# Two handovers from routed experts to wide-headed attention: rooms of the gathers, order of the first two tiles, place of a weight product

## The chip, the core and the metric

The kernel runs on one core of a Trainium2 chip. A core has five engines that work side by side: TensorE (PE in the profile; its weight loads are PEld), VectorE (DVE), ScalarE (ACT), GpSimd (POOL) and SyncE (SP), which here only issues transfers. Each engine takes its instructions in order from a queue of its own. Sixteen DMA engines move data between the device memory and the on-chip memory. The metric is the device time of one execution in microseconds; smaller is better.

## What is computed

The reference is a network of four layers over 16 sequences of 64 tokens with 256 features (1024 token rows), with a context of 1024 keys of 192 features per sequence. Each layer has a cross attention to the context, a mixing step along the sequence and a feed-forward part, each added to `x`:

```python
x = x + _L1_ffn_ref(_layernorm(x), ...)     # 8 experts, each token goes to one
x = x + _L2_xattn_ref(_layernorm(x), ctx)   # 8 heads of 64
x = x + _L2_attn_ref(_layernorm(x), ...)    # a linear recurrence
x = x + _L2_ffn_ref(_layernorm(x), ...)     # 8 experts, each token goes to two
x = x + _L3_xattn_ref(_layernorm(x), ctx)   # 8 heads of 64
x = x + _L3_attn_ref(_layernorm(x), ...)    # a state-space layer
x = x + _L3_ffn_ref(_layernorm(x), ...)     # three dense products
```

Two pieces matter here. A routed layer adds to each token the outputs of its experts, weighed by gates. And the state-space layer maps its input `u` to a step size through two matrices one after the other:

```python
x_dbl = u @ x_proj_w
delta, b, c = jnp.split(x_dbl, [D_INNER, D_INNER + D_STATE], axis=-1)
delta = jax.nn.softplus(delta @ dt_proj_w + dt_proj_b)
```

The first 512 columns of `x_proj_w` (called xT, transposed) and `dt_proj_w` (dt), both 512 x 512, can be multiplied with each other once, without any token. The kernel does that: this is the weight product.

## The kernel before

The 1024 token rows lie on chip as `xs`, eight tiles of 128 rows (NT = 8); a tile holds two sequences. The layers run one after the other; the two cross attentions with eight heads of 64 (L2 and L3) share one routine, `heads64` (line 420), and each is woven with the sequence layer that follows it: L2 with a recurrence, L3 with the state-space layer (`state_space`, line 1779).

*Experts to attention.* In a routed layer (`L1_ffn`, `L2_ffn` at line 1397) each expert's output rows `yb` are written to a buffer `ys` in the device memory, on ACT's DMA queue (lines 1328 and 1460). Nothing is added to `xs` there. The attention that follows does it, tile by tile, in `carry` (line 1306): for each chosen expert it allocates a tile, gathers 128 rows of `ys` into it with an indirect DMA on POOL's queue (line 1304), and adds them, times the gate, to `xs` on DVE (line 1313). After L1's experts a tile has one such gather, after L2's experts two. In `heads64` the gathers' room has the tag `o` with one buffer, the same buffer that then holds the tile's normalized rows (lines 450 and 452).

*`heads64`.* `output_matrices` (line 429) multiplies value and output weights per head. `normalized(i)` (line 449) carries tile i, normalizes it (statistics on DVE, a power on POOL at line 160, scaling on DVE at line 453), transposes it on TensorE (line 179) and copies the result (`hT`). `queries(i)` (line 458) multiplies `hT` by the query weights and scales them to `qT` on DVE (line 465). `with_keys(i, n)` (line 472) multiplies the queries by the key weights, for n = 0 and 1, and copies the result to `qp`. Then come 32 steps, each a tile, one of its two sequences and half of the heads: `scores` (line 500) makes two 128 x 1024 score tiles, `exp_rows` takes their maxima on DVE (line 223) and exponentials on ACT (line 225) into tiles of the tag `p` (two buffers of 1024 numbers per row), which later steps transpose and average. Before the change the prologue runs in this order:

```python
            output_matrices()
            for i in range(2):
                normalized(i)
            queries(0)
            for n in range(2):
                with_keys(0, n)
```

Tiles 2 and on are normalized inside the steps, two tiles ahead.

*What sets the order.* TensorE's instructions run in the order in which the program writes them (`manual_schedule`). The other engines' queues are ordered by a scheduler that works with estimated times, so an instruction may stand well ahead of its place in the program. It keeps data and rooms: a tile whose tag has all buffers taken waits until an older one has had its last reader.

*Between the steps.* `heads64` calls `breathe(place)` four times a step, which is the `go` function of the neighbouring layer. In L3 the state-space layer's first piece of work is `weights()` (line 1806): its first call takes the weights, the next four make one quarter each of the weight product, xT by dt on TensorE (line 1813), which a copy on ACT puts in xT's place (line 1814). So two quarters run before the first scores and two behind them. `prepare` (line 1817) uses the product once two tiles have left the attention.

*Weights.* Weights are loaded into a ring of two slots (`slot`, `carve`, `load` at line 131, on SP's queue); `pack` hands out a slot and starts the loads of the next. `pack_L3_attn` (line 1733) loads five matrices of the state-space layer when the last L2 expert has left its slot: in, xT, dt (1024 KB each), bc (64 KB) and out (512 KB). Each L2 expert's weights are three loads of 1024 KB. The pool `act` has two rooms of 8 KB per row, `htok` and `hT`, which hold the normalized tokens and their transpose while `L2_ffn` routes; in L3 `hT` next holds `up` (line 1831) and `htok` holds `bc_rep`.

Of the kernel before, what the change touches and what calls it, by code (L numbers as in the profile page):

```python
# [11 lines left out]
F32 = mybir.dt.float32  # L12
# [30 lines left out]
class Net:  # L43
# [373 lines left out]
            nc.sync.dma_start(ck, self.a["ctx"][b])  # L417
        return cT, ck

    def heads64(self, large=None, breathe=lambda place: None, finished=lambda i: None):  # L420


        nc = self.nc
# [23 lines left out]
                self.evict(wvo2[:, 2 * g : 2 * g + 2], ps)  # L447

        def normalized(i):
            self.carry(i, "o", 1)  # L450
            mv, rs = self.norm_tile(self.xs[:, i, :], 1e-5)
            o = self.lp.tile([128, D], F32, tag="o", bufs=1, name="o")
            nc.vector.tensor_scalar(o, self.xs[:, i, :], mv[:, 0:1], rs, ALU.subtract, ALU.mult)
            nc.gpsimd.tensor_tensor(self.xs[:, i, :], self.xs[:, i, :], bo, ALU.add)
            hT[i] = self.lp.tile([128, 2, 128], F32, tag="hT", bufs=2, name="hT")
            self.evict(hT[i], self.transposed(o))
# [15 lines left out]
        def with_keys(i, n):  # L472

            qT, qp = qpT[i]
            ps = [large([128, 4, 2, S]) for _ in range(2)]
            for hp in range(4):
                for r in range(2):
                    rows = slice(64 * r, 64 * r + 64)
                    self.mm(
                        ps[r][:, hp].rearrange("p b q -> p (b q)"),  # L480
                        [(wkT[rows, hp, 128 * n : 128 * n + 128], qT[rows, hp, :])],
                    )
            for r in range(2):
# [49 lines left out]

        with self.tc.manual_schedule(engines={mybir.EngineType.PE}):
            output_matrices()
            for i in range(2):
                normalized(i)
            queries(0)
            for n in range(2):
                with_keys(0, n)  # L540
            steps = [(i, par, g) for i in range(NT) for par in range(2) for g in range(2)]
            one = two = None
            for k in range(len(steps) + 2):
                x = steps[k] if k < len(steps) else None
                now = None
                if x is not None:
                    i, par, g = x
                    if not par and not g:
                        onT = [
                            self.lp.tile([128, 8, 2, S], F32, tag="onT", bufs=1, name="onT"),  # L550
                            self.lp.tile([128, 4, 2, S], F32, tag="onT2", bufs=1, name="onT2"),
                        ]
                    if not g:
                        ctx = self.fetch_cut_ctx(2 * i + par)
                    now = {"x": x, "ctx": ctx, "onT": onT}
                breathe(0)
# [12 lines left out]
                breathe(3)  # L569
                if two is not None:  # L570
                    by_features(on, two["onT"], two["x"][1], 2 * two["x"][2] + 1)
                if one is not None:
                    one["on"] = averages(one["pT"][0], one["sums"][0], one["ctx"][1])
                if two is not None and two["x"][1:] == (1, 1):
                    output(two["x"][0], two["onT"])
                    finished(two["x"][0])
                if now is not None and (par, g) == (0, 1):
                    if i + 2 < NT:
                        normalized(i + 2)
                    if i + 1 < NT:  # L580
                        queries(i + 1)
                one, two = now, one
# [720 lines left out]
    def gather_rows(self, out, src, at):  # L1303
        return self.nc.gpsimd.indirect_dma_start(out, None, src, bass.IndirectOffsetOnAxis(ap=at, axis=0))

    def carry(self, i, tag="back", bufs=2):

        if self.routed is None:
            return
        for at, g in zip(self.routed.at, self.routed.gates):  # L1310
            y = self.lp.tile([128, D], F32, tag=tag, bufs=bufs, name="back")
            self.gather_rows(y, self.ys, at[:, i : i + 1])
            self.nc.vector.scalar_tensor_tensor(
                self.xs[:, i, :], y, g[:, i : i + 1], self.xs[:, i, :], ALU.mult, ALU.add
            )
# [81 lines left out]
    def L2_ffn(self):  # L1397
# [31 lines left out]

        for e in range(E):  # L1430
            w1, w2, w3 = self.pack()
            dT = self.lp.tile([128, 2, CAP], F32, tag="dT", bufs=2, name="dT")
            for v, (s0, n) in enumerate(L2_CUTS):
                hb = self.lp.tile([n, D], F32, tag=f"hb{n}", bufs=2, name="hb")
# [296 lines left out]


    def pack_L3_attn(self):
        self.slot()
        return tuple(self.load(f"L3a_{n}") for n in ("in", "xT", "dt", "bc", "out"))

    def pack_L3_ffn(self):
        t = self.ring.tile([128, 4 * RING], U8, tag="w", name="w")
# [8 lines left out]
    def L3(self, ctx_pool):  # L1747
        tc, nc = self.tc, self.nc
        with ExitStack() as stack:
# [10 lines left out]
            with (  # L1760
                tc.tile_pool(name="sb_L3x", bufs=1, side="left", reuse_waits="tile") as self.lp,
                tc.tile_pool(name="ps_L3x", bufs=1, space=PSUM, reuse_waits="tile") as self.lps,
            ):
                self.heads64(
                    lambda shape: self.lps.tile(shape, F32, tag="t", bufs=2, name="large"),
                    ssm.go, ssm.more,
                )
            ctx_pool.__exit__(None, None, None)
            self.lp = pool("sb_L3f", bufs=1, side="left")
# [9 lines left out]
    def state_space(self):  # L1779
        nc = self.nc  # L1780
        N = 16
        w = []
# [20 lines left out]
            s.xn += 1  # L1803
            return s.x[s.xn % 6]

        def weights():
            w.extend(self.pack(ahead=False))
            yield

            for k in range(4):  # L1810
                cols = slice(k * 128, (k + 1) * 128)
                ps = self.lps.tile([128, 4, 128], F32, tag="t", bufs=2, name="large")
                self.mm(ps.rearrange("p m f -> p (m f)"), [(w[1][:, r, cols], w[2][:, r, :]) for r in range(4)])
                nc.scalar.copy(w[1][:, :, cols], ps)
                yield

        def prepare(k):
            win, wdt, _, wbc, _ = w
            ug = ugs[k % 2]
            os = []  # L1820
            for t in range(2):
# [66 lines left out]
            return got  # L1888

        def items(k):  # L1890
            wout = w[4]
            ug = ugs[k % 2]

            bc = self.act.tile([128, 2, 4, CHUNK], F32, tag="htok", name="bc_rep")
# [83 lines left out]
        def more(i):  # L1978
            s.ready = i + 1

        s.go, s.more = go, more
        s.x = rooms(self.sb, "x", 6)
        s.rep = rooms(self.sb, "rep", 4)
        s.xn = s.repn = 0
# [321 lines left out]
```

## Time and profile before

| | us |
|---|---|
| median of 3 runs | 3025.43 |
| lowest and highest | 3025.0, 3040.91 |
| the profiled execution | 3029.32 |
| its span | 3027.5 |
| TensorE busy, of the span | 2704.1 (89%) |
| VectorE busy | 1482.0 (49%) |
| ScalarE busy | 1022.6 (34%) |
| GpSimd busy | 309.4 (10%) |
| mean granted TensorE clock | 0.942 |

The page gives busy time by engine, the span in forty slices, and the chain of work that ended last, followed back from the last instruction to whatever released each step. The other views used below are the timeline (instructions in order of time, with the idle time of the engine before each and what ended it) and windows (busy time of every engine in a stretch, the granted clock, the share of the DMA engines and their rate). Times in them are counted from the span's start. The handover from L1's experts to L2's attention lies at about 1302 to 1331 us, the one from L2's experts to L3 at about 2025 to 2090 us.

### The profile page before, as it was taken

Reading aid. Unit: us, or ns where it says so; the run is one execution under the profiler, and the core shown is the slowest. Engines: PE = TensorE matmul, PEld = TensorE weight load, DVE = VectorE, ACT = ScalarE, POOL = GpSimd, SP = SyncE. Lnnn points to the kernel's source line nnn. Section 1 sums busy time; section 2 is a strip of 40 time slices with the busy share of each in tenths; the row PEclk is TensorE's granted clock in tenths of the full one; section 3 lists DMA queues with packets and bytes.
Section 4 is the critical chain, followed back from the end, with each engine's and each line's share of the span. In section 5 each row is a group of like instructions: output and inputs, shape, how many; then the busy total and the mean of one; then the engine's idle time right before and its main releaser. Section 6 shows DMA issues by size and latency. Waiting matters only on the chain.

```text
span 3027.5 us, 42618 instructions
## 1 busy us (share of the span) xinstructions
PE 2704.1 (89%) x16840; PEld 1955.0 (65%) x16840; DVE 1482.0 (49%) x3177; ACT 1022.6 (34%) x2290; POOL 309.4 (10%) x428
## 2 busy tenths in 40 slices
PE   7888997999999787979999997887998898887899
PEld 3566784666666346857777776874766666665668
DVE  3654115666666643234444344223445657658581
ACT  2331122555555111223333321122335455455330
POOL 1112223000000112310101011201001000000000
PEclk9997997999999897989999998998999999998999
DMA  9504771101010004811111113450212212121110
GB/s 242 171 27 159 253 230 51 36 26 36 26 36 22 28 9 171 281 49 54 55 44 47 60 42 116 163 217 22 67 43 84 74 51 83 56 67 53 57 36 7
DMA packets 79220, 253.55 MB, mean 84 GB/s; under 512 B 15151, under 2 KB 26954, under 8 KB 69290
## 3 DMA queue, kind: packets, MB, share of 16 engines
q1 hardware_dynamic: 59562, 165.01, 17.5%
q0 software_dynamic: 13312, 80.28, 7.8%
q10 hardware_dynamic: 6144, 5.51, 0.5%
q8 instruction: 134, 2.20, 0.3%
q14 instruction: 68, 0.56, 0.1%
HBM read 233.80 MB, written 14.82 MB: 82 GB/s over the span
## 4 chain that ended last, share of the span: by engine, by line
PE 64%; DVE 11%; ACT 4%; DMA 3%; issue 3%; POOL 1%; SPq 1%; ACTq 0%; DVEq 0%; POOLq 0%
PE misc L69 11%; PE sc L500 8%; PE halves L69 7%; PE gu L69 5%; PE misc L235 4%; PE ps_h L69 4%; PE po L69 4%; PE ps_t L235 3%; PE sc L69 2%; PE misc L864 2%; ACT p L225 2%; PE o L915 2%; PE misc L878 2%; DMA back<-ys,route_at 2%; DVE x L1926 2%
## 5 line engine op out<-in xcount | busy, mean ns | idle before, releaser
L223 DVE TENSOR_REDUCE nmx<-sc 128x1 f32<-128x1024 f32 x264 | 311.6, 1218 | 234.9 <-PE sc L500 150.4
L225 ACT ACTIVATE p<-sc,nmx 128x1024 f32<-128x1024 f32 x264 | 294.6, 1116 | 312.1 <-DVE nmx L223 311.4
L500 PE MATMUL sc<-ctxT,qp 128*128 128x512 f32 (+1 forms) x1024 | 353.4, 599 | 0.0
L500 PEld LDWEIGHTS sc<-ctxT,qp 128*128 128x128 f32 (+1 forms) x1024 | 137.8, 189 | 153.0 <-issue 151.6
L69 PE MATMUL halves<-ctx,pT 128*128 128x192 f32 x1024 | 191.0, 343 | 9.4 <-DVE xs L89 4.0
L69 PEld LDWEIGHTS halves<-ctx,pT 128*128 128x128 f32 x1024 | 178.4, 203 | 12.3 <-DVE xs L89 4.5
L160 POOL TENSOR_TENSOR ln_rs<-ln_ve,nhalf 128x1 f32<-128x1 f32 x120 | 67.0, 563 | 1142.3 <-DVE ln_ve L158 1081.6
L69 PE MATMUL misc<-ctx,pT 128*128 128x192 f32 x1024 | 177.6, 327 | 0.5 <-DVE qT L465 0.5
L69 PEld LDWEIGHTS misc<-ctx,pT 128*128 128x128 f32 x1024 | 166.3, 191 | 2.1 <-DVE qT L465 1.0
L235 PE MATMUL ps_t<-ident,p 128*128 128x128 f32 x1088 | 147.2, 277 | 21.9 <-ACT p L225 14.0
L1916 ACT ACTIVATE da<-rep,al 128x252 f32<-128x252 f32 x256 | 114.7, 498 | 115.0 <-DVE x L1926 95.6
L1926 DVE TENSOR_TENSOR_SCAN x<-da,x 128x512 f32<-128x512 f32 x128 | 151.9, 1210 | 1.9 <-ACT da L1916 1.4
L235 PE MATMUL misc<-ident,p 128*128 128x128 f32 x1024 | 139.8, 283 | 14.1 <-ACT p L225 6.7
L237 ACT COPY pT<-ps_t 128x512 f32<-128x512 f32 x182 | 104.3, 585 | 139.3 <-PE ps_t L235 137.3
L235 PEld LDWEIGHTS ps_t<-ident,p 128*128 128x128 f32 x1088 | 127.1, 143 | 36.0 <-ACT p L225 17.7
L235 PEld LDWEIGHTS misc<-ident,p 128*128 128x128 f32 x1024 | 112.2, 143 | 40.2 <-ACT p L225 13.3
L69 PE MATMUL ps_h<-r,w 128*128 128x256 f32 x512 | 115.3, 385 | 0.0
L237 ACT COPY pT<-misc 128x512 f32<-128x512 f32 x128 | 75.0, 586 | 114.9 <-PE misc L235 114.6
L69 PEld LDWEIGHTS ps_h<-r,w 128*128 128x128 f32 x512 | 97.8, 192 | 16.6 <-issue 2.9
L69 PE MATMUL gu<-dT,wa 128*128 128x128 f32 (+1 forms) x864 | 104.7, 280 | 3.7 <-ACT dT L64 2.4
L239 DVE COPY pT<-misc 128x512 f32<-128x512 f32 x128 | 88.2, 689 | 39.4 <-PE misc L235 28.9
L69 PE MATMUL po<-wb,hid 128*128 128x256 f32 (+1 forms) x440 | 105.9, 388 | 0.2 <-ACT hid L1380 0.2
(468 smaller groups left out, 4449.5 us busy)
## 6 DMA issues: line engine op xcount, KB each, us to landing
ctx<-in_ctx SPq DMA_DIRECT2D x48, 768.0 KB
ctxT<-in_ctxT SPq DMA_DIRECT2D x48, 512.0 KB
w<-in_L2f_W SPq DMA_DIRECT2D x24, 1024.0 KB
rep<-dus SPq DMA_DIRECT2D x256, 64.0 KB
ctxT<-in_ctxT SPq DMA_DIRECT2D x16, 768.0 KB
ctxT<-in_ctxT SPq DMA_DIRECT2D x96, 128.0 KB
ys<-yb ACTq DMA_DIRECT2D x40, 128.0 KB
bc_rep<-bcs SPq DMA_DIRECT2D x32, 128.0 KB
```

The source lines that it names most:

```text
L69: self.nc.tensor.matmul(out, lhsT, rhs, start=n == 0, stop=n == len(pairs) - 1)
L160: nc.gpsimd.tensor_tensor(rs, ve, self.nhalf, ALU.pow)
L223: self.nc.vector.tensor_reduce(nmx, sc, AX.X, ALU.max, negate=True)
L225: self.nc.scalar.activation(p, sc, AF.Exp, bias=nmx, accum_out=sums)
L235: self.nc.tensor.transpose(ps[:, u, :], p[:, at : at + 128], self.ident)
L237: self.nc.scalar.copy(pT[:, 4 * g : 4 * g + 4, :], ps)
L239: self.nc.vector.tensor_copy(pT[:, 0:4, :], ps)
L500: nc.tensor.matmul(sc[u][:, bass.ts(kh, 512)], qp[n][par][rows, h : h + 2, :].rearrange("p h q -> p (h q)"), ctx[0][rows, at], start=n == ...
L864: nc.tensor.matmul(ps[kh], wk[:, kh, cols], cT[:, bass.ts(kh, 512)], start=True, stop=False)
L878: nc.tensor.matmul(ps[kh][:, u, :], cT[:, 512 * kh + at : 512 * kh + at + 128], wv[:, 0, :], start=u == 0, stop=False,)
L1916: nc.scalar.activation(da[:, g, :, 1:], now[j][:, 0, :].rearrange("p (b s) -> p b s", s=S)[:, :, 1:], AF.Exp, scale=al[:, col : col + 1],)
L1926: nc.vector.tensor_tensor_scan(flat, da.rearrange("p g b s -> p (g b s)"), flat, 0.0, ALU.mult, ALU.add)
```

## The change

Four edits, cut to their core:

1. `carry` can be given a room. For the first two tiles of `heads64` the gathers go into a tile of the exponentials' tag `p`, seen as four rows of 256, each expert's rows in a part of its own. Tiles from the third on keep the tag `o` with one buffer.
2. In the prologue tile 1 is normalized behind tile 0's queries and their products with the keys, instead of ahead of them.
3. `heads64` calls a new hook, `first`, between the output matrices and tile 0. In L2 it does nothing. In L3 it makes the whole weight product, which was spread over the first steps.
4. xT and dt are loaded in `L2_ffn`, in the program's place of the fourth expert, into the rooms `htok` and `hT` of the pool `act`. `pack_L3_attn` only carves its slot; in, bc and out are loaded by the first call of `weights()`. The slot no longer has a part for dt.

```diff
         def normalized(i):
-            self.carry(i, "o", 1)
+            if i < 2:
+                self.carry(i, self.lp.tile([128, 4, D], F32, tag="p", bufs=2, name="p"))
+            else:
+                self.carry(i, tag="o", bufs=1)
...
             output_matrices()
-            for i in range(2):
-                normalized(i)
+            first()
+            normalized(0)
             queries(0)
             for n in range(2):
                 with_keys(0, n)
+            normalized(1)
...
-    def carry(self, i, tag="back", bufs=2):
+    def carry(self, i, room=None, tag="back", bufs=2):
...
-        for at, g in zip(self.routed.at, self.routed.gates):
-            y = self.lp.tile([128, D], F32, tag=tag, bufs=bufs, name="back")
+        for n, (at, g) in enumerate(zip(self.routed.at, self.routed.gates)):
+            y = self.lp.tile([128, D], F32, tag=tag, bufs=bufs, name="back") if room is None else room[:, n, :]
...
         for e in range(E):
             w1, w2, w3 = self.pack()
+            if e == 3:
+                self.early = [
+                    self.act.tile([128, 4, 512], F32, tag=tag, name=name)
+                    for tag, name in (("htok", "w_xT"), ("hT", "w_dt"))
+                ]
+                for w, n in zip(self.early, ("xT", "dt")):
+                    nc.sync.dma_start(w, self.a[f"L3a_{n}"])
...
     def pack_L3_attn(self):
         self.slot()
-        return tuple(self.load(f"L3a_{n}") for n in ("in", "xT", "dt", "bc", "out"))
+        shape = {n: self.a[f"L3a_{n}"].shape for n in ("in", "bc", "out")}
+        return self.carve(*shape["in"]), self.carve(128, 4, 512), self.carve(*shape["bc"]), self.carve(*shape["out"])
...
-        def weights():
+        def first():
             w.extend(self.pack(ahead=False))
-            yield
-
+            x, dt = self.early
             for k in range(4):
                 cols = slice(k * 128, (k + 1) * 128)
                 ps = self.lps.tile([128, 4, 128], F32, tag="t", bufs=2, name="large")
-                self.mm(ps.rearrange("p m f -> p (m f)"), [(w[1][:, r, cols], w[2][:, r, :]) for r in range(4)])
+                self.mm(ps.rearrange("p m f -> p (m f)"), [(x[:, r, cols], dt[:, r, :]) for r in range(4)])
                 nc.scalar.copy(w[1][:, :, cols], ps)
-                yield
+
+        def weights():
+            for n, to in zip(("in", "bc", "out"), (w[0], w[2], w[3])):
+                nc.sync.dma_start(to, self.a[f"L3a_{n}"])
+            yield
```

More of the change, by code (lines that the diff above doesn't have):

```diff
@@ L418, in fetch_cut_ctx, with heads64 @@
         return cT, ck
-    def heads64(self, large=None, breathe=lambda place: None, finished=lambda i: None):
+    def heads64(
+        self, large=None, breathe=lambda place: None, finished=lambda i: None, first=lambda: None
+    ):
         nc = self.nc
@@ L1765, in L3 @@
                     lambda shape: self.lps.tile(shape, F32, tag="t", bufs=2, name="large"),
-                    ssm.go, ssm.more,
+                    ssm.go, ssm.more, ssm.first,
                 )
@@ L1812, in weights @@
                 ps = self.lps.tile([128, 4, 128], F32, tag="t", bufs=2, name="large")
[L1813 removed]
+                self.mm(ps.rearrange("p m f -> p (m f)"), [(x[:, r, cols], dt[:, r, :]) for r in range(4)])
                 nc.scalar.copy(w[1][:, :, cols], ps)
[L1815 removed]
+        def weights():
+            for n, to in zip(("in", "bc", "out"), (w[0], w[2], w[3])):
+                nc.sync.dma_start(to, self.a[f"L3a_{n}"])
+            yield
         def prepare(k):
[L1818 removed]
+            win, wdt, wbc, _ = w
             ug = ugs[k % 2]
@@ L1890, in items @@
         def items(k):
-            wout = w[4]
+            wout = w[3]
             ug = ugs[k % 2]
@@ L1979, in more @@
             s.ready = i + 1
-        s.go, s.more = go, more
+        s.go, s.more, s.first = go, more, first
         s.x = rooms(self.sb, "x", 6)
```

## The prediction

> **What bounds the kernel now.** I read the page's busy line and chain first, then the chain in order of time, which points at two stretches where no matmul is on it, and then the timeline of those two.
>
> ```profile
> PE 2704.1 (89%) x16840; PEld 1955.0 (65%) x16840; DVE 1482.0 (49%) x3177; ACT 1022.6 (34%) x2290; POOL 309.4 (10%) x428
> ...
> PE 64%; DVE 11%; ACT 4%; DMA 3%; issue 3%; POOL 1%; SPq 1%; ACTq 0%; DVEq 0%; POOLq 0%
> ```
>
> TensorE is busy 89% of the span and carries 64% of the chain that ends last, so microseconds in which it stands idle, or does work that fits into an idle stretch, are what an edit can win. Two such stretches lie where a routed layer hands over to attention. The timeline of the second (L2's experts to L3):
>
> ```profile
> 2030.05 1.94 PE L69 MATMUL large<-w 64*64 64x256 f32 x16 [0.71 <-DVE w L62]
> ...
> 2036.07 0.97 POOL L1304 DMA_INDIRECT back<-ys,route_at  x1 [76.02 <-DMA w<-in_L3a_bc]
> ...
> 2039.58 0.94 POOL L1304 DMA_INDIRECT back<-ys,route_at  x1 [2.54 <-DVE xs L1313]
> ...
> 2044.99 0.69 PE L179 MATMUL halves<-ident,o 128*128 128x128 f32 x2 [13.00 <-DVE o L453]
> ...
> 2054.88 0.69 PE L179 MATMUL halves<-ident,o 128*128 128x128 f32 x2 [9.20 <-DVE o L453]
> ...
> 2055.36 3.62 PE L69 MATMUL large<-hT,w 128*128 128x128 f32 x16
> ...
> 2063.16 0.48 DVE L1313 SCALAR_TENSOR_TENSOR xs<-back,route_g,xs 128x256 f32<-128x256 f32 x1 [3.35 <-DMA back<-ys,route_at]
> ...
> 2067.43 9.88 PE L69 MATMUL large<-w 128*128 128x512 f32 x16 [0.59 <-ACT qp L64]
> ...
> 2077.15 5.51 PE L500 MATMUL sc<-ctxT,qp 128*128 128x512 f32 x16
> ...
> 2082.59 7.13 PE L69 MATMUL large<-w 128*128 128x512 f32 x16
> ```
>
> Columns: start, duration, engine, line, output<-input, and in brackets the idle time and its releaser. The output matrices end at 2031.99. TensorE then waits 13.00 us for tile 0's normalized rows and 9.20 us for tile 1's, and only then multiplies queries. Each tile's two gathers go one behind the other: the second waits for the add that frees the single room (2036.07, 2039.58). After the waiting come 9.88 and 7.13 us of a matmul that depends on no token: the weight product (L1813), around the first scores. The stage's windows (busy us by engine, granted clock, DMA share, GB/s):
>
> ```profile
> 1953.00:1967.00 14.00, 13.85 (x104) 13.53 (x103) 3.19 (x10) 3.21 (x11) 3.30 (x5) 1.00 0.65 250
> ...
> 2030.00:2036.00 6.00, 1.94 (x16) 1.03 (x16) 0.79 (x2) 0.79 (x2) 0.00 (x0) 0.95 1.01 412
> ...
> 2045.00:2055.00 10.00, 0.80 (x3) 0.40 (x4) 2.57 (x7) 0.00 (x0) 3.33 (x5) 0.50 0.09 26
> 2055.00:2067.00 12.00, 7.54 (x50) 6.79 (x50) 3.77 (x11) 1.08 (x3) 3.85 (x5) 0.64 0.08 23
> ```
>
> At 2030 to 2036 the DMA engines are full (1.01, 412 GB/s): 3.74 MB of state-space weights, issued at 2025.16, stand beside the last expert's rows that the first gather needs. The clock falls to 0.50 while TensorE waits. The first handover (L1's experts to L2), from its timeline:
>
> ```profile
> 1304.66 0.95 POOL L1304 DMA_INDIRECT back<-ys,route_at  x1 [24.93 <-issue]
> ...
> 1312.42 0.66 PE L179 MATMUL misc<-ident,o 128*128 128x128 f32 x2 [1.98 <-DVE ang_y L1632]
> ...
> 1315.66 1.04 POOL L1304 DMA_INDIRECT back<-ys,route_at  x1 [2.58 <-issue]
> ...
> 1321.15 0.66 PE L179 MATMUL misc<-ident,o 128*128 128x128 f32 x2 [8.07 <-DVE o L453]
> ...
> 1321.60 3.62 PE L69 MATMUL misc<-hT,w 128*128 128x128 f32 x16
> ...
> 1330.99 6.25 PE L500 MATMUL sc<-ctxT,qp 128*128 128x512 f32 x16
> ```
>
> Queries (1321.60) wait for tile 1's transposes (1321.15), though tile 0's were ready at 1312.42: tile 1's gather starts only at 1315.66.
>
> **The change part by part.** I work out each handover as one chain on TensorE, since the three edits there overlap.
>
> *L2.* Now from tile 0's transposes to scores: 1312.42 to 1330.99. After it, tile 1's transposes stand behind `with_keys`. Tile 0's end at 1313.08, their copy at 1313.54. Tile 1's gather is now issued early and sits on POOL's queue beside the two powers of L1612 and L1615, and its add and statistics on DVE before tile 0's scaling. Bounds: 0 (it fits gaps) to 2.2 (1.26 us for one more gather on POOL, the spacing at which the L1 experts' row gathers follow each other, 1249.93 and 1251.19; 0.95 for an add and statistics on DVE); I take 1.0, as DVE was busy 4.71 us of 1306 to 1313. So 1314.5; queries 3.62; 0.05+0.68 for qT (L465), 0.1 to the keys; from the keys' first matmul to scores 4.47 (1326.52 to 1330.99); tile 1's transposes 0.66. Sum: 1324.1. Gain 1330.99-1324.1 = **6.9** (5.7 to 7.9). Rooms: the exponentials' tiles have two buffers, emptied by the adds long before the first exponential asks for one; no wait. Tile 2's gather waits for tile 1's transposes to free `o`, now near 1324; it is needed after the second scores, over 15 us later, so nothing.
>
> *L3.* Removed from the path: both waits and both product pieces. Added: the product right behind the output matrices. From 2031.99: product 2x7.08 = 14.2 (the chain's figure for the warm half) to 2046.2; meanwhile tile 0's gathers, adds and scaling run. Even with the first gather as late as now, 2036.07, the second starts 1.26 behind it, lands 2.73 later and the rows are scaled by 2042.6, 3.6 us before 2046.2; with 2 MB less in front of it the gather should start some 4 to 5 us earlier. That is why the paired rooms cost and win nothing here: the product covers them (without it they are worth the 2.3 us between 3.5 and 1.26). Then transposes 0.4, copy 0.5, queries 1.80 (the same sixteen matmuls at full clock at 2100.76), qT 0.75, keys to scores 4.47, tile 1's transposes 0.4: scores start at 2054.5 instead of 2077.15. To the next scores it is 9.8 us (L2's 10.55 from 1330.99 to 1341.54, less the 0.7 by which its first scores ran longer than 5.51): 2064.3 instead of 2092.39. Gain 28.1.
>
> A new wait goes against it. Tile 2's two gathers still share `o`: free at 2054.5, first gather 2054.8, lands 2057.5, second 2058.3, lands 2061.0, add done 2061.5. DVE runs in order, and that add was queued ahead of the key copies (2063.16 above). If it stands ahead of the first maximum, wanted at 2060.0, that is 1.5 late, and exponential, transposes and second scores with it. Bounds 0 to 2.3 (with statistics too); I take 1.5, as the queue now has it so. L3: **26.6**.
>
> *The moved loads.* xT and dt (two DMAs, 2.1 MB) go to SP in the expert stage, in places that are free once the router has read them. Queues other than TensorE's are ordered by the scheduler: line 1832's memset for L3 ran at 1885.04, 140 us ahead of its layer, so these may come early too, between the second and third expert's weights, where the engines stand nearly idle (1895 to 1910: share 0.11). If they follow the fifth expert's: row 1953 moves 250 GB/s x 14 us = 3.5 MB a period, plus 2.1 is 5.6 MB; at the 412 GB/s of row 2030 that takes 13.6 of the 14.4 us of an expert. [...] The row is this chip's; I take 0 and keep 1.3. The three loads left (in, bc, out, 1.6 MB) move behind the first `go`; the first matmul on them comes after 2237, when two tiles are finished. The four ACT copies of the product, 0.59 each, fall where ACT is idle.
>
> *POOL.* The `up` memsets of L1832 now wait for the product, since dt holds their room. Behind one on POOL could stand tile 0's power (then transposes are 1.3 late) or a gather (9 late). The gathers have what they need some 10 us before the product ends; I take 0.
>
> *Clock.* Row 2030 grants 0.95 although TensorE works only a third of it, so I price the product warm. [...] The gaps here are 0.7 us, [...], 9.88 for 7.08: 2.8 less gain. I keep it for the range.
>
> Sum: 6.9+26.6 = 33.5. The profiled execution took 3029.32 (span 3027.5), 3.9 over the median of the runs, 3025.43; I carry the gain over unchanged: **3025.4-33.5 = 2992**.
>
> **The rivals.** *Part is given back (20%).* The order of DVE, ACT, POOL and SP is planned anew, and a gather or memset lands in front of a power, a maximum or a copy at both handovers: 9+2.3+1.3+2.8 off, and a few microseconds in L3's mixed stage, leaves 12 to 22: about 3008. For: six adds waited 23.0 us for gathers in this handover. Against: TensorE's order is written by hand and every producer has 3 to 10 us of slack.
>
> *The change does not do what it says (8%).* If the early weights come late, or scores wait for something that the views hide (L2's odd 2.58 us in front of the gather at 1315.66 has no releaser), only L2's part or less remains: 3011 to 3025, no change that can be told.
>
> *Slower (4%).* One mechanism: with shifted estimates the scheduler puts a state-space scan (L1926, 1.21 us) in front of the attention maxima on DVE. L3 has 32 steps with two maxima each, some 24 beside running scans: 24x2x1.21 = 58, net +24: 3050. It decides from 49 us lost, about 1.0 us per maximum. Against: DVE is in the chain with 11% and both kernels hold the same work; its order should repeat.
>
> **How the numbers follow.** The first case has 68%, 2984 to 3002 by the bounds: down 1.0 (L2), 1.5 (the add not in the way) and 5, up 1.2 (L2), 2.8 (cold product), 1.3 (loads) and 5, where the 5 stand for the new order of the planned queues over the 970 us that follow. About 0.5%, 15 us, is what a measurement here tells from no change, so faster means under 3010.3. The second case is about two thirds below it (3001 to 3013). Faster: 0.68+0.14 = 0.82; same: 0.06+0.08 = 0.14; slower: 0.04. The range runs from the first case's lower end through nearly all of the second: 2984 to 3012.
>
> **What would show it.** Right: the product's thirty-two matmul rows start near 2032 at 7.1 us per sixteen, no gap above 2 us between them and the first scores near 2054; second scores near 2064; L2's first scores near 1324; expert periods still 14.4 us; everything later shifted by the same amount. Wrong: a gap ahead of the product (weights late), a gap behind it (gathers or a POOL wait), expert periods longer, or L3's later stage longer than now by more than 10 us.

## The result, and the profile after

| | before | after |
|---|---|---|
| median of 4 runs each, us | 3027.23 | 2998.26 |
| lowest and highest | 3025.0, 3040.91 | 2992.45, 2999.23 |
| ratio, 95% interval | | 0.9889 (0.9862 to 0.9917) |
| the profiled execution, us | 3029.32 | 2998.29 |
| its span | 3027.5 | 2996.5 |
| mean granted TensorE clock | 0.942 | 0.948 |

By the ratio the change wins 33.6 us (25 to 42), by the two profiled executions 31.0. The forecast was 33.5. That they agree to 0.1 us is in part luck: by the traces L3's handover brought 26.9 and L2's 1.4 to 5.3, so 28 to 32 together, and the interval is 17 us wide. One of the forecast's two terms was right, the other mis-sized.

The page's busy line and chain of the kernel after:

```profile
PE 2700.2 (90%) x16840; PEld 1952.8 (65%) x16840; DVE 1482.1 (49%) x3177; ACT 1022.7 (34%) x2290; POOL 308.7 (10%) x428
...
PE 15%; DVE 6%; ACT 3%; DMA 2%; issue 1%; SPq 1%; POOL 0%; DVEq 0%; ACTq 0%; POOLq 0%
```

The same instructions run for the same time (PE 4 us less); what shrank is idle time. The chain adds up to some 30% of the span only: it was followed less far than before's, and its shares can't be set beside those of before. The timeline of L3's handover, after:

```profile
2027.71 14.00 PE L69 MATMUL large<-w_dt,w_xT 128*128 128x512 f32 x32
...
2029.16 0.96 POOL L1312 DMA_INDIRECT p<-ys,route_at  x1 [73.03 <-DMA ys<-yb]
...
2030.43 0.95 POOL L1312 DMA_INDIRECT p<-ys,route_at  x1 [0.31 <-issue]
...
2037.05 0.41 DVE L460 TENSOR_SCALAR o<-xs,ln_mv,ln_rs 128x256 f32<-128x256 f32 x1 [0.29 <-POOL ln_rs L160]
...
2041.55 0.38 PE L179 MATMUL halves<-ident,o 128*128 128x128 f32 x2
...
2042.49 2.02 PE L69 MATMUL large<-hT,w 128*128 128x128 f32 x16 [0.56 <-ACT w L1832]
...
2048.81 0.44 PE L179 MATMUL halves<-ident,o 128*128 128x128 f32 x2
2049.08 5.52 PE L507 MATMUL sc<-ctxT,qp 128*128 128x512 f32 x16
...
2056.01 0.49 DVE L1321 SCALAR_TENSOR_TENSOR xs<-back,route_g,xs 128x256 f32<-128x256 f32 x1 [0.99 <-DMA back<-ys,route_at]
...
2056.87 1.21 DVE L223 TENSOR_REDUCE nmx<-sc 128x1 f32<-128x1024 f32 x1
...
2061.14 6.27 PE L507 MATMUL sc<-ctxT,qp 128*128 128x512 f32 x16
```

The waits of 13.00 and 9.20 us are gone. In their place stands the whole product, 14.00 us without a gap, and tile 0's rows are scaled at 2037.05, 4.5 us before TensorE comes to transpose them. The gathers now follow each other at 1.27 us. Its windows (start and end, length, busy us and count of PE, PEld, DVE, ACT and POOL, granted clock, DMA share, GB/s):

```profile
2028.00:2034.00 6.00, 6.00 (x15) 2.65 (x15) 1.20 (x3) 1.00 (x2) 3.80 (x4) 1.00 0.25 68
2034.00:2049.00 15.00, 12.72 (x70) 7.65 (x70) 4.57 (x14) 2.70 (x7) 2.69 (x6) 1.00 0.03 9
...
1949.00:1963.00 14.00, 13.92 (x105) 13.61 (x103) 3.20 (x10) 3.24 (x11) 3.29 (x5) 1.00 0.65 249
```

The DMA engines, full at this place before, are a quarter busy. The clock, 0.50 in the waits before, stays at 1.00. The expert stage (last row) moves what it moved before. L2's handover, after:

```profile
1307.71 1.03 POOL L1312 DMA_INDIRECT p<-ys,route_at  x1 [1.71 <-issue]
...
1314.09 0.66 PE L179 MATMUL misc<-ident,o 128*128 128x128 f32 x2 [4.48 <-DVE ang_y L1648]
...
1315.37 3.54 PE L69 MATMUL misc<-hT,w 128*128 128x128 f32 x16 [0.62 <-issue]
...
1319.69 1.16 PE L69 MATMUL misc<-qT,w 64*128 64x128 f32 x16 [0.78 <-DVE qT L472]
...
1321.77 2.40 PE L69 MATMUL misc<-qT,w 64*128 64x128 f32 x16 [0.91 <-DVE qp L62]
...
1325.16 7.32 PE L507 MATMUL sc<-ctxT,qp 128*128 128x512 f32 x16
...
1335.72 1.94 PE L235 MATMUL ps_t<-ident,p 128*128 128x128 f32 x8 [0.44 <-DVE av_r L519]
...
1337.46 6.30 PE L507 MATMUL sc<-ctxT,qp 128*128 128x512 f32 x16
```

The 8.07 us in front of tile 1's transposes are gone and its gather starts at 1307.71. But look at the durations: the two products with the keys are the same sixteen matmuls and take 1.16 and 2.40 us; the first scores take 7.32, where L3's take 5.52. The granted clock was 0.50 from 1308.31 to 1318.55 and from 1321.96 to 1328.79.

**How the traces are compared.** Executions of one kernel already differ before the change is reached: at the end of L1's experts (their last matmul starts at 1301.24 in before) the profiled executions below stand between -0.5 and +9.2 us against before, although TensorE has the same work up to there; nearly all of it arises in the first 200 us. So each handover is measured from the end of its own experts: the start of a kernel's scores, less the start of its last expert matmul ahead of them, against the same in before (negative is earlier). All these readings are of one profiled execution each.

| us, from the experts' end | L2 first | second | third scores | L2's last scores | L3 first | second | third scores |
|---|---|---|---|---|---|---|---|
| after | -5.3 | -3.4 | -2.6 | -1.4 | -23.8 | -26.9 | -26.1 |
| L2's handover alone | -4.1 | -2.1 | -2.1 | +1.1 | -0.7 | -0.7 | -0.7 |
| L3's handover alone | 0.0 | 0.0 | 0.0 | 0.0 | -23.9 | -26.9 | -26.4 |
| product in steps | -4.1 | -2.0 | -0.9 | +0.4 | -16.0 | -16.0 | -16.0 |
| loads with the ring | -4.1 | -2.1 | -2.1 | -1.2 | -16.0 | -19.8 | -19.8 |
| old rooms | -4.9 | -4.3 | -4.3 | -4.2 | -20.3 | -23.9 | -23.9 |
| old order | -4.2 | -3.8 | -3.8 | -3.2 | -23.4 | -28.2 | -28.2 |
| old rooms and old order | -0.2 | +0.1 | +0.2 | 0.0 | -10.4 | -14.2 | -14.2 |
| one cure in each | -4.8 | -3.2 | -2.5 | -1.9 | -23.6 | -28.4 | -28.4 |
| own room, third tile | -4.4 | -2.6 | -2.5 | -1.6 | -23.1 | -27.7 | -27.6 |
| own room, all later tiles | -4.4 | -2.1 | -1.5 | -0.4 | -11.1 | -9.4 | -7.9 |
| four unused matmuls | -5.4 | -3.7 | -3.0 | -2.9 | -22.9 | -26.8 | -26.8 |
| two unused matmuls | -8.1 | -7.0 | -6.5 | -6.6 | -23.8 | -26.9 | -26.4 |

L3's columns are firm: the four executions with the same L3 (after, L3 alone, both with unused matmuls) agree within 0.2 us at the second scores. L2's are not: the four with the same L2 (after, L2 alone, product in steps, loads with the ring) differ by 1.2 us at the first scores and by 2.5 at the last, and after is the best of them.

### The profile page after: what moved, and what is told of

The parts are those of the page before. It is cut to its first block, busy times and chain, and to the rows that moved or that the text cites. A ratio compares the mean times of both kernels' runs of the same rounds, so it can differ in the third digit from the quotient of the medians.

```text
span 2996.5 us, 42608 instructions
## 1 busy us (share of the span) xinstructions
PE 2700.2 (90%) x16840; PEld 1952.8 (65%) x16840; DVE 1482.1 (49%) x3177; ACT 1022.7 (34%) x2290; POOL 308.7 (10%) x428
## 5 line engine op out<-in xcount | busy, mean ns | idle before, releaser
L235 PE MATMUL misc<-ident,p 128*128 128x128 f32 x1024 | 139.8, 283 | 14.2 <-ACT p L225 6.7
```

Source lines behind the costliest of these rows:

```text
L235: self.nc.tensor.transpose(ps[:, u, :], p[:, at : at + 128], self.ident)
```

## The experiments

Ratios below are times against before, with their 95% intervals; the kernel after has 0.9889. A difference of two such ratios has both intervals in it, some 9 to 11 us either way. So by their times only both cures undone (experiment 4), the rooms for all later tiles (7) and, barely, the product in the steps (2) are clear of after; the smaller differences rest on the traces.

**1. Each handover alone.** In `heads64` the new rooms and order hang on the layer; for L2 alone, L3 also gets its product in the steps and its five loads back.

```diff
+        wide = large is not None
...
-            if i < 2:
+            if i < 2 and not wide:
...
+            if not (not wide):
+                normalized(1)
             queries(0)
             for n in range(2):
                 with_keys(0, n)
-            normalized(1)
+            if not wide:
+                normalized(1)
```

(For L3 alone the two conditions are the other way round.)

> The first handover (L1's experts to L2's attention) is as in the changed kernel; the second (L2's experts to L3) is as before: tile 1 ahead of tile 0's queries, tag o for the first two tiles, the weight product in steps, all five loads in the ring. By the forecast's sum the gain is 6.9 us (about 0.9977 of before). The theory from the changed kernel's trace (the granted clock goes to half in windows of 3.4 us that now fall on the prologue and the first scores) says: first scores some 5.3 us earlier, second some 3.4, and 1.5 to 4 us at the end (0.9987 to 0.9995). A rival: L2's edits interact with L3's and are worth 0 or less alone; then first scores are not more than 1 us earlier.

> The second handover alone is as in the changed kernel; the first is as before. By the forecast's sum the gain is 26.6 us (0.9912 of before). From the changed kernel's trace the same: L3's first scores stand 23.9 us, its second 26.9 us earlier than L2's offset there, so 26 to 28 us. The rival (a part of the changed kernel's 31 us came from elsewhere, say from a different order of the planned queues in L2): 23 us or less.

L2 alone: 0.9984 (0.9975 to 0.9993), 4.8 us (2.1 to 7.6). L3 alone: 0.9901 (0.9878 to 0.9923), 30.0 us (23 to 37). They add up to 34.8, the whole change has 33.6: neither needs the other. L3's scores are as forecast (26.9 by the trace). L2's are nearer to the second theory (4.1 and 2.1 at the first two scores, where it had 5.3 and 3.4), and its time holds both that and the forecast's 6.9.

A caution goes with it: in L2 alone, where L3's program is that of before, the stage from L3's tenth scores to the end ran 4.5 us shorter than in before. That much one execution's total can be off.

**2. The product back in the steps**, early loads kept.

```diff
         def first():
+            pass
+
+        def weights():
             w.extend(self.pack(ahead=False))
...
+            yield
             x, dt = self.early
             for k in range(4):
...
                 nc.scalar.copy(w[1][:, :, cols], ps)
+                yield
```

> The changed kernel, early loads and all, but the weight product is made in the steps again, two quarters ahead of the first scores and two behind them. By the forecast's working the product costs 14 to 17 us on the path again, and what stands in its place is tile 0's chain alone, whose transposes can then come near 2037 instead of 2041.6: 9 to 13 us slower than the changed kernel. If the product is hidden wherever it stands (rival), the two are equal.

0.9922 (0.9907 to 0.9938), 10.0 us above after; L3's second scores 10.8 later, within the 9 to 13 expected. Its timeline:

```profile
2042.99 0.69 PE L179 MATMUL halves<-ident,o 128*128 128x128 f32 x2 [9.72 <-DVE o L460]
...
2044.20 3.78 PE L69 MATMUL large<-hT,w 128*128 128x128 f32 x16 [0.52 <-DVE hT L62]
...
2054.78 7.77 PE L69 MATMUL large<-w_dt,w_xT 128*128 128x512 f32 x16
...
2062.38 5.51 PE L507 MATMUL sc<-ctxT,qp 128*128 128x512 f32 x16
...
2067.82 7.13 PE L69 MATMUL large<-w_dt,w_xT 128*128 128x512 f32 x16
```

The wait for tile 0 (9.72) is back and the product (7.77 and 7.13) stands behind it. The queries take 3.78 us instead of 2.02: from 2034 to 2049, with that wait in it, the granted clock was 0.55, in after 1.00. So the product in the idle stretch not only hides itself, the clock also stays up for what follows: 1.76 on the queries and 1.8 on the keys' two products (2.08 and 2.40 against 1.16 and 1.49), about a third of the 10.8.

**3. xT and dt loaded with the ring slot**, behind the last expert, the product still ahead.

```diff
-            if e == 3:
-                self.early = [
...
-                for w, n in zip(self.early, ("xT", "dt")):
-                    nc.sync.dma_start(w, self.a[f"L3a_{n}"])
...
+        return tuple(self.load(f"L3a_{n}") for n in ("in", "xT", "dt", "bc", "out"))
```

> The changed kernel, but xT and dt are loaded with the ring slot again, behind the last expert, as before. If the early loads are what lets the product stand ahead of tile 0, the product waits for its two weights, which land near 2031, 3.5 us after the 2027.7 of the changed kernel, and the last experts' rows land near 2031 as well, not 2028.2: 3.5 to 8 us slower than the changed kernel. If the loads only go elsewhere and nothing waits for them (rival), the time is the changed kernel's within 1 us.

0.9917 (0.9895 to 0.9938), 8.5 us above after; L3's second scores 7.1 later. Its timeline:

```profile
2035.71 16.93 PE L69 MATMUL large<-w 128*128 128x512 f32 x32 [3.78 <-DMA w<-in_L3a_dt]
2035.94 0.97 POOL L1312 DMA_INDIRECT p<-ys,route_at  x1 [75.75 <-DMA w<-in_L3a_bc]
```

The product waits for its weight (3.78), and then takes 16.93 us in place of 14.00, since the clock was at half from 2034.84 to 2041.67: 3.8 and 2.9 make 6.7 of the 7.1. The first gather is 2.6 us later too, counted from the experts' end, but the longer product covers it. The rival, that nothing waits for these loads, is out.

**4. Old rooms, old order, and both.**

```diff
-            if i < 2:
+            if False:
...
-            normalized(0)
+            for i in range(2):
+                normalized(i)
             queries(0)
             for n in range(2):
                 with_keys(0, n)
-            normalized(1)
```

The first line is the old rooms, the rest the old order.

> The changed kernel, but the gathers of the first two tiles use the single room o again. The forecast said that the paired rooms win nothing in L3, since the product covers tile 0's two gathers: 0 us. A second theory: with one room, tile 1's gathers cannot start before tile 0's transposes (2041.9 us) free it, and its transposes, which stand between the keys and the first scores, come 2 to 6 us later than the 2048.8 of the changed kernel; the whole is then 2 to 6 us slower than the changed kernel. In L2, where tile 1 has one gather, first scores 0 to 3 us later.

> The changed kernel, but tile 1 is normalized ahead of tile 0's queries again, in both handovers. By the forecast's sum the order is what L2 wins (6.9 us) and in L3, with its rooms and the product's cover, 1 to 3 us: 8 to 10 us slower than the changed kernel. By the clock theory L2 keeps only 1.5 to 4 us of its gain, and this kernel is 2 to 6 us slower. The rival, that the early gather of tile 1 (its own room) is what counts and not the order: 0 to 1 us slower.

> The changed kernel with both the single room o for the first two tiles and the old order (tile 1 ahead of tile 0's queries); the product ahead and the early loads stay. Undone one at a time, the rooms cost about 3 us at L3's second scores and nothing in L2, and the order nothing in either handover. If the two are separate costs, both undone cost about 3 us against the changed kernel. If they are two cures of one wait (tile 1's rows behind tile 0's), so that each covers for the other, L2 loses its whole 4 us at the scores, and in L3 tile 1's gathers start only at tile 0's transposes (about 2042), which puts the queries near 2050 in place of 2042.5: 8 to 12 us slower than the changed kernel in all.

Old rooms: 0.9906 (0.9885 to 0.9926), 5 us above after; in L3 second scores 3.0 later, in L2 nothing lost. Old order: 0.9881 (0.9866 to 0.9895), the same as after, so that of its three expectations the rival's came; second scores of L3 stand even 1.3 earlier, and experiment 5 repeats that (1.5). Both: 0.9962 (0.9948 to 0.9976), 22 us above after, more than the 8 to 12 expected; L2 loses all, L3 12.7, about 16 together by the traces. The timeline of both undone:

```profile
2047.98 0.38 PE L179 MATMUL halves<-ident,o 128*128 128x128 f32 x2
...
2049.03 1.00 POOL L1312 DMA_INDIRECT back<-ys,route_at  x1 [0.59 <-issue]
...
2057.97 0.69 PE L179 MATMUL halves<-ident,o 128*128 128x128 f32 x2 [9.60 <-DVE o L460]
```

Tile 1's first gather waits for tile 0's transposes to free the room, and TensorE then stands 9.60 us, as it did before. With either cure alone the wait is gone. With the new order and old rooms that gather is as late, but queries and keys run meanwhile (the timeline of the old rooms):

```profile
2042.89 1.00 POOL L1312 DMA_INDIRECT back<-ys,route_at  x1 [0.59 <-issue]
...
2049.28 0.48 DVE L1321 SCALAR_TENSOR_TENSOR xs<-back,route_g,xs 128x256 f32<-128x256 f32 x1 [2.50 <-DMA back<-ys,route_at]
...
2050.16 2.40 PE L69 MATMUL large<-qT,w 64*128 64x128 f32 x16 [2.11 <-DVE qp L62]
...
2052.49 0.69 PE L179 MATMUL halves<-ident,o 128*128 128x128 f32 x2
```

Tile 1's transposes follow the keys at once. What is lost is lost ahead of them: tile 1's adds, waiting for their gathers, stand on VectorE in front of the copies `qT` and `qp`, for which TensorE waits 2.07 and 2.11 us in place of 0.83 and 0.88; and the second product with the keys takes 2.40 in place of 1.49, as it did in L2 of after, where 0.54 was granted over it.

With the new rooms and old order, tile 1's rows are ready when TensorE comes (the timeline of the old order):

```profile
2051.96 0.44 PE L179 MATMUL halves<-ident,o 128*128 128x128 f32 x2 [0.84 <-DVE o L460]
2052.23 1.95 PE L69 MATMUL large<-hT,w 128*128 128x128 f32 x16
```

Two edits, one wait. Undone one at a time they look worth 3 us and nothing; undone together they are worth the whole gain in L2 (3.4 at the second scores) and 12.7 us in L3.

**5. One cure in each handover**: in L2 the order with old rooms, in L3 the rooms with the old order.

> The changed kernel with, of the two cures, only one in each handover: in L2 the new order with the single room o, in L3 the paired rooms with the old order. From the runs before: L2 keeps 4.2 us of its scores' gain to the end of its attention in place of 1.4 (no half-clock window at the second scores), and L3's second scores stand 28.3 us earlier than its experts' end in place of 26.9: 2 to 4.5 us faster than the changed kernel at the start of L3's third scores. If the differences were accidents of the run (rival), equal to the changed kernel; in the time alone the 0.1% may not be told.

0.9890 (0.9871 to 0.9909), the same as after. L3's part came as expected (-28.4). L2's did not: -1.9 and not -4.2 at its last scores, although that program's L2 is the one of the old rooms. The clock was at half from 1337.82 to 1341.23, over the second scores (from 1335 to 1345 0.83 was granted); in the run of the old rooms it was at full from 1328.50 on (1.00 from 1335 to 1345). With that stretch on the second scores L2 kept 1.9, without it 4.2. So the expected 2 to 4.5 us at L3's third scores came from L3 alone (2.3).

**6. Unused matmuls in L2's gap.** In L2 `first` gets four (then two) matmuls whose result nobody reads; no other work changes.

```diff
+            def warm():
+                ps = self.misc([128, 512])
+                for _ in range(4):
+                    self.nc.tensor.matmul(ps, self.ident, self.ctx[0].rearrange("p t d -> p (t d)")[:, :512], start=True, stop=True)
-            self.heads64(breathe=lru.go, finished=lru.more)
+            self.heads64(breathe=lru.go, finished=lru.more, first=warm)
```

> The changed kernel with four more matmuls, identity by 512 columns of the context, ahead of tile 0 in L2's handover, where TensorE stands idle; nothing uses their result. If the shrinking of L2's gain (6.9 forecast, 5.3 at the first scores, 3.4 at the second) is due to half-clock windows, the pattern of windows moves: with more of 1314 to 1337 at full clock the second scores come 1 to 3 us earlier. [...] If the clock is not the cause, the windows may move but scores do not.

> The changed kernel with two in place of four of the unused matmuls ahead of tile 0 in L2's handover. With four, queries and keys ran at full clock (about 3.3 us less), but tile 0's transposes stood 2.6 us late behind them, and the first scores came out even. If the clock theory holds, two fill the window as well but end some 2.5 us earlier: first scores 1 to 2.5 us earlier, after the experts' end, than in the changed kernel. [...]

Four: 0.9884 (0.9864 to 0.9904). They took 5.26 us and tile 0's transposes stood 2.6 us late behind them; queries and keys ran at full clock (2.05, 1.16 and 1.49 us against 3.54, 1.16 and 2.40 in after) and won it back. The second scores came 0.3 us earlier than in after, not the 1 to 3 expected. Two: 0.9873 (0.9852 to 0.9894), median 2991.85. The timeline with two:

```profile
1311.93 1.98 PE L1617 MATMUL misc<-ctx,ident 128*128 128x512 f32 x4 [1.23 <-DVE w L62]
...
1314.39 0.41 PE L179 MATMUL misc<-ident,o 128*128 128x128 f32 x2 [0.47 <-DVE ang_y L1654]
...
1315.37 2.05 PE L69 MATMUL misc<-hT,w 128*128 128x128 f32 x16 [0.57 <-DVE hT L62]
...
1320.28 1.49 PE L69 MATMUL misc<-qT,w 64*128 64x128 f32 x16 [0.91 <-DVE qp L62]
...
1322.75 5.52 PE L507 MATMUL sc<-ctxT,qp 128*128 128x512 f32 x16
```

One of its windows:

```profile
1311.00:1322.00 11.00, 7.09 (x54) 4.97 (x54) 5.71 (x23) 3.32 (x9) 2.50 (x4) 0.99 0.21 73
```

The same window of the kernel after:

```profile
1311.00:1322.00 11.00, 5.59 (x36) 4.87 (x36) 5.37 (x20) 1.85 (x6) 2.50 (x4) 0.66 0.01 1
```

With 1.98 us of extra work the stretch is granted 0.99 in place of 0.66, the first scores start 2.8 us earlier (1 to 2.5 were expected) and take 5.52 us instead of 7.32, and L2 keeps 6.6 us to its last scores. This is the fastest kernel of the study by its trace (span 2992.5 against 2996.5) and by its median; the intervals of the two ratios overlap, so the times alone don't tell it from after.

Could these two matmuls merely have met the clock's stretches at a good place? The run with a room for the third tile alone (experiment 7) is a control that has none of them. Its clock falls 6.69 us after the start of its last expert matmul, as with two unused matmuls (there it was 0.50 from 1307.77 to 1311.19), and rises 3.41 us later, also as there; but from 1318.32 to 1335.39 it is at half again, where with two 1.00 was granted from 1311.19 to 1331.67. Its timeline:

```profile
1319.10 3.75 PE L69 MATMUL misc<-hT,w 128*128 128x128 f32 x16 [0.96 <-ACT cos L1660]
...
1330.11 8.14 PE L509 MATMUL sc<-ctxT,qp 128*128 128x512 f32 x16
```

Its first two scores stand at -4.4 and -2.6, against -8.1 and -7.0, although its tile 0 was ready 0.4 us earlier. The four have such neighbours too: in L2 alone and in the loads with the ring the clock falls 7.13 and 7.16 us after that matmul, with the four 7.21, and the scores stand at -4.1 and -2.1, against -5.4 and -3.7.

**7. Rooms for the tiles from the third on** (the ring is 128 numbers per row smaller for it): one buffer for all of them, then for the third tile alone.

```diff
-                self.carry(i, tag="o", bufs=1)
+                self.carry(i, tag="back", bufs=1)
```

> The changed kernel, but the tiles from the third on gather into a room of their own (tag back, one buffer, the ring slot 128 numbers per row smaller), not into o. If the waits for o (tile 2's second gather, the add that stands ahead of a maximum on VectorE, losses of 0.3 to 0.7 us at several later steps of L2) cost what the trace of the changed kernel suggests, this is 1 to 4 us faster than it. If the next term on the path is late by as much anyway, 0. If the new order of the planned queues costs more than the waits do, slower.

> The changed kernel, but the third tile alone (i = 2) gathers into a room of its own (one buffer), all later tiles into o. With such a room for all later tiles, the gathers and adds of many tiles were queued ahead of tile 0's copies and maxima, and L3's scores came 13 to 19 us later. If it was the later tiles' adds, this kernel does not have them ahead, and the third tile's add leaves the first two maxima alone: second scores of L3 0 to 2 us earlier than in the changed kernel. If one tile's adds in front of the copies are enough for the loss (rival), L3's first scores are over 3 us later.

For all: 0.9945 (0.9932 to 0.9958), 17 us slower than after, where 1 to 4 faster was hoped for. Its timeline:

```profile
2053.69 0.96 POOL L1312 DMA_INDIRECT back<-ys,route_at  x1 [2.98 <-DVE xs L1321]
...
2057.11 0.48 DVE L1321 SCALAR_TENSOR_TENSOR xs<-back,route_g,xs 128x256 f32<-128x256 f32 x1 [2.82 <-DMA back<-ys,route_at]
...
2058.03 3.75 PE L69 MATMUL large<-hT,w 128*128 128x128 f32 x16 [11.57 <-issue]
```

Freed from the wait for `o`, the gathers and adds of later tiles were planned ahead of tile 0's own copies. Each waits 2 to 4 us for the one room, the copies stand behind them on VectorE, and TensorE stands 11.57 us. In after the wait for `o` holds them back. For the third tile alone: 0.9900 (0.9881 to 0.9918), the same as after; the two first maxima now run as one pair (in after an add that waits for its gather stands between them):

```profile
2059.43 2.36 DVE L223 TENSOR_REDUCE nmx<-sc 128x1 f32<-128x1024 f32 x2 [4.80 <-PE sc L509]
...
2064.38 5.52 PE L509 MATMUL sc<-ctxT,qp 128*128 128x512 f32 x16
```

From the first scores (2053.86) to the second it is 10.52 us, against 12.06 in after: 1.5 us less (half clock costs some 0.9 in after, where the transposes take 1.97 in place of 1.09; here as much is lost on the first scores, whose maximum starts 5.57 us behind their start in place of 4.71), of which the second scores keep 0.8, since the first stood 0.7 later in this run.

## Why the prediction was right or wrong

*L3's handover, 26.6: right, 26.9 measured.* The product runs at full clock (14.00, forecast 14.2), right behind the output matrices; the weights and gathers have what they need well before it ends. The scores came 1.2 us earlier than summed, 1.0 of it in the keys: from them to the scores the forecast carried over 4.47 us from L2, half of it at half clock (0.50 from 1328.89 to 1332.30 in before), and at full clock (1.00 from 2034 to 2049) it took 3.47 to tile 1's transposes. The step to the second scores took 12.06 us, where 9.8 and 1.5 were forecast, 0.8 more, part of it the transposes behind the maxima (1.97 us, 0.50 granted from 2059.24 to 2062.65). That the two misses nearly cancel is luck. The 1.5 for the third tile's add is what experiment 7 measured.

*L2's handover, 6.9: mis-sized.* It brought 5.3 at the first scores, 3.4 at the second and 1.4 at its last; in the three other executions with the same L2, 4.1, 2.0 to 2.1, and between a gain of 1.2 and a loss of 1.1. Two terms of the sum failed:
- The 1.0 for POOL and VectorE ahead of tile 0 was too small: queries start 1.4 us later than its 1314.5, counted from the experts' end, so the term was 2.4, just over its upper bound of 2.2. Tile 1's gather at 1307.71 stands on POOL between the two powers that the forecast named, and TensorE's wait for tile 0 ends behind VectorE's work on them. Where L2 has the old rooms (experiments 4 and 5) and that gather comes later, tile 0's transposes start 11.2 us after the start of the last expert matmul, as in before; in after it is 13.4.
- The gain at the first scores was taken to last, as if the step to the second stayed that of before. The chain of before has, in order of time:

```profile
1340.48 1.06 PE ps_t L235 x8
1341.54 5.35 PE sc L500 x16
```

From 1330.99 that is 10.55 us (10.39 by the timeline, where the second scores start at 1341.38). In after it took 12.30, with first scores of 7.32 in place of 6.25 and transposes of 1.94 in place of 1.06; 0.75 was granted over those scores and 0.50 over those transposes. That carrying over the cadence of a stretch also carries its clock was not seen. Experiment 6 and its control show the clock as the cause: two matmuls that compute nothing used bring 8.1 and 7.0.

To sum the two L2 edits as one chain was right; that either alone removes the wait (experiment 4) was not said.

The last fall, from 2.6 to 1.4, comes in three small steps of 0.2 to 0.7 at later scores, where an add that waits for its gather stands ahead on VectorE; that is read from the trace and was not tried by itself. At the end of L2's experts the offset of after stands at -3.7 again, in other runs with the same L2 at -2.9, -1.9 and +0.2. This part of the scatter stays open.

*Rooms cost and win nothing in L3: wrong by 3.0 us.* The product covers tile 0's gathers, as argued. But tile 1's cannot start before tile 0's transposes free `o` (2042.89), and then its adds stand in front of the copies for the keys (experiment 4). The forecast followed the product's cover for tile 0 and never priced tile 1 in the old room, though it priced an add in such a place for the third tile.

*The loads, 0: right.* They were issued at 1883.48 and 1884.16, right behind the second expert's weights, just ahead of the idle place named in the forecast, so the fuller period of 5.6 MB that it priced never arose; what such a period takes, and with it the 1.3 us kept for the range, was not shown. The gain from moving them was in the L3 sum, and experiment 3 prices it at 7.1.

*The clock.* Pricing the product warm was right: 1.00 was granted over all its 14.00 us. The 2.8 us kept for the range was the author's estimate, from before's two pieces of the product (9.88 us, and 7.08 by its chain), and did not come. In L2 the clock fell with no long wait just ahead of it: at 1321.96, after 3.41 us in which TensorE was busy 1.71 us and its longest pause was 0.91 (two windows of after):

```profile
1318.55:1321.96 3.41, 1.71 (x20) 1.33 (x20) 1.36 (x3) 0.65 (x2) 0.00 (x0) 1.00 0.02 5
1321.96:1325.37 3.41, 2.90 (x19) 2.60 (x19) 0.92 (x3) 0.74 (x2) 0.00 (x0) 0.50 0.00 0
```

*POOL's memset, 0: right.* It waited until 2041.83, just behind the product, and what follows it on POOL is at 2042.79, in time. *The rivals:* no step of "part is given back" happened in L3. In L2 a gather did land in front of a power, as this rival had it, but cost only 1.4 us more than priced; with the clock, 3.5 us of the 6.9 were gone by the second scores and 5.5 by the last. The slower rival's scans ahead of the maxima are not seen: L3's offset at the end is within 1 us of that at its third scores.

## What to carry to other kernels

Independent work that waits behind a stall belongs into the stall: here it hid itself, and the clock stayed up for what followed (1.00 from 2034 to 2049, 0.55 with the product in the steps). When two edits cure one wait, undo both before judging either. And a duration carried over from the old trace carries its clock with it (the same sixteen matmuls of the queries took 2.02 and 3.78 us): look whether the same instruction has two durations before using one.

## What the runs showed of the hardware

In the traces of before and after the granted clock is 1.00 or 0.50. In after it was 0.50 from 1308.31 to 1318.55, 1.00 to 1321.96, 0.50 to 1328.79, 1.00 to 1335.62 and 0.50 to 1339.03: stretches of 10.24, 3.41, 6.83, 6.83 and 3.41 us, each a whole multiple of 3.41. So are all others of these two executions, the stretch at the very end of each apart, and those read above in the experiments: 6.83 (loads with the ring), 17.07 (third tile's room), 3.41 (one cure in each).

How busy TensorE was in the 3.41 us before a change didn't decide by itself: in after the clock fell to 0.50 behind such a window with 3.14 us busy (1871.53 to 1874.94) and stayed at 1.00 behind one with 1.38 (2619.00 to 2622.41). What does decide was not shown.

From the start of the last expert matmul to the clock's fall in L2's handover it was 7.60 us in after, 7.17 in before, 7.13 in L2 alone and 7.16 in the loads with the ring. The same L2 brought 5.3 us at its first scores in after and 4.1 in L2 alone and in the loads with the ring.
